# A two-layer graph network on one core: matmul sums parted at other places around transposes, identity products between TensorE's waits, a second copy of layer 1's table, and node rows written later

## The chip, the cores and the metric

The kernel runs on one core of a Trainium2 chip. The metric is the device time of one execution in microseconds (us), as the median of several runs.

## What is computed

A graph of N = 6250 nodes (256 features) and E = 200000 edges, sorted by destination, goes through two graph attention layers (4 heads of 64, then 1 head of 256). Cut to one layer:

```python
te  = relu(edge_attr @ We + be) * exp(x @ Wo + bo)[src][:, None]      # one row per edge
hx  = x @ Wg                                                          # one row per node
al  = leaky_relu((hx·a_s)[src] + (hx·a_d)[dst] + (te @ Wge)·a_e, 0.2)
al  = exp(al - segment_max(al, dst)[dst]); al = al / segment_sum(al, dst)[dst]
out = segment_sum(hx[src] * al, dst) + b                              # also a self loop per node
x   = relu(out + x)            # layer 1: no relu, and the inputs are added once more
```

Layer 1 reads hx of layer 0's result at each edge's source, and a source can be any node: layer 1's first gather needs, in principle, the last node row that layer 0 makes.

## The kernel before

**Steps.** The edges are cut into 66 steps a layer: 64 of 24 chunks of 128 edges, then one of 14 and one of 13. A step covers a window of at most M = 112 consecutive nodes. Its number in the whole run is k (0 to 65 in layer 0, 66 to 131 in layer 1), in its layer s. Within a step:

- `gather` (L941): GpSimd issues one indirect DMA per chunk; it fetches the 128 source rows of the chunk from the layer's table in DRAM, `T[0]` or `T[1]`, into the step's tile G. Three G buffers rotate by k mod 3.
- `rphase1` (L1041, L1042), `rphase2` (L1050), `adst` (L1167), `edge_rows` (L1181): the edges' own term, by TensorE and ScalarE, turned to rows by VectorE.
- `logits` (L1195 to L1212): VectorE adds the terms and scans for maxima; it needs the step's last gather.
- `ends` (L1219), `links` (L1229, L1231, L1236), `maxima` (L1246 to L1272): a small transpose on TensorE, scans across partitions, a transpose back, and the exponentials.
- `scale` (L1303): VectorE multiplies the gathered rows by the weights, in pieces given by `cuts`; `carried` (L1285 to L1293) adds what the step before left over for its last node.
- `onehots` (L1132) and `sums` (L1322): one-hot matrices S, and per chunk one product S x G that accumulates in the PSUM tile u (two matmul instructions a chunk). `evict` (L1327) copies u to U.
- `finish` (L1338 to L1409 in layer 0): merges the self loop, makes the node's new x (tile fb) and, last, in two additions (L1407, L1409), the node row that layer 1 will add to its result.
- `rows1` (two transposes, L1415, and a copy, L1417), `rows2` (the table row's product, L470), `rows3`: VectorE adds the bias (L474), ScalarE takes an exponential (L1427), and SyncE's queue (SP) writes the 112 rows to `T[1]` (L1456), the node rows to `nd` (L1458), and one element to the step before's `nd` (L1461).

**Order.** The schedule is written by hand: instructions run on each engine in the order in which the program lists them, and each waits for its operands and buffers by semaphores. Every step but the last three of a layer goes through the loop in `edges`. The last three (called a, b and c here: 24, 14 and 13 chunks) go through `ending`, in which a's sums stand among b's logits and links, b's sums among c's, and the node rows of a, b and c come last. `after` is the step that follows: the first of layer 1 at the turn, and none at the end of the kernel.

**The turn.** After a's sums, `ending` lets the first step of layer 1 gather already (24 early gathers, L941) from `T[1]`, although the rows of a, b and c are not in it. For the sources that are missing, `lacking` (at k = 4) filled the table's last rows, `sources` loads the list of sources, `select` (L1102, twice) compares it with the numbers of the last 256 nodes, `lack_rows` (L1110) reads these 256 rows of `T[1]` when they are there, and `complete` (L1120, L1121) adds the missing rows to G, 24 pieces of four matmul instructions and one VectorE instruction each. The step after that (k = 67) gathers from the whole `T[1]`; the one after (k = 68) takes a buffer that holds the list and one of the two select matrices until `complete` is done.

**End.** The last two steps of layer 1 write their rows by an indirect DMA of GpSimd (L1469). `flag` sums up the checks of the input (L926 to L930); `general` at the end branches on it.

Of the kernel before, what the change touches and what calls it, by code (L numbers as in the profile page):

```python
# [22 lines left out]
F32 = mybir.dt.float32  # L23
# [8 lines left out]
P = 128  # L32
# [47 lines left out]
class Kernel:  # L80
# [10 lines left out]
    def run(self):  # L91
# [4 lines left out]
        self.T = [self.dp.tile([N + P, L.TW], F32, name=f"T{L.l}") for L in self.L]  # L96
        n, w = (self.NS + 1) // 2, self.L[1].TW + D
# [580 lines left out]
    def edges(self, ctx):  # L678
# [31 lines left out]
        for k, st in enumerate(steps):  # L710
# [63 lines left out]
        self.flag()  # L774
# [8 lines left out]

    def ending(self, a, b, c, pv, late, after):

        nc, k = self.nc, a["k"]
        self.load_lb(k + 3)
# [28 lines left out]
        self.sums(a, (0, n // 3))  # L816
# [7 lines left out]
        self.sums(a, (n // 3, n // 2))  # L824
        self.links(b)
        self.sums(a, (n // 2, n))
        early = after and self.early
# [36 lines left out]
        drain(self.scale(c, cuts=(1, 1 + m // 2, m)))  # L864
# [22 lines left out]
        self.rows2(b)  # L887
        f = self.finish(c)
# [7 lines left out]
        if early:  # L896
            self.select(after, 0)
        self.rows3(c)
        if after:
            fill = iter(())  # L900
            if early:
                self.lack_rows(after)
                self.select(after, 1)
# [5 lines left out]
            for _ in range(C // 3):  # L909
                next(fill, None)  # L910
# [4 lines left out]
            for _ in range(C // 3):  # L915
                next(fill, None)
# [15 lines left out]
    def gather(self, st):  # L932
# [7 lines left out]
        for c in range(0) if st["k"] == 0 and self.CX > last else range(last + 1) if own else (last, *range(last)):  # L940
            nc.gpsimd.indirect_dma_start(  # L941
                out=G[:, c, 0:L.TW], out_offset=None, in_=self.T[L.l][0:self.N, :],
# [130 lines left out]
    def lacking(self):  # L1073
# [4 lines left out]
        for n in (N - 2 * P, N - P):  # L1078
            nc.sync.dma_start(self.T[1][n:n + P, :], none)
# [20 lines left out]
    def select(self, st, j):  # L1100

        self.nc.vector.tensor_tensor(st["sel"][j], st["row"], self.k_lack[:, j:j + 1].to_broadcast([P, C * P]),  # L1102
                                     op=OP.is_equal)
# [210 lines left out]
    def sums(self, st, *parts):  # L1314
        nc, L, c = self.nc, st["L"], st["C"]
        G, S = st["G"], st["S"]
        for a, b in parts or ((0, c),):
            for i in range(a, b):
                j = st["n"] = st.get("n", -1) + 1
                if j == 0:  # L1320
# [54 lines left out]
    def nodes0(self, st, wp, e=None):  # L1375
# [6 lines left out]
        hw = wp.tile([P, D], F32, name="hw", bufs=2)  # L1382
        self.nc.scalar.activation(hw, xw, AF.Relu, bias=tw[:, L.ln + 1:L.ln + 2],
                                  scale=tw[:, L.ln:L.ln + 1])
        st["hw"] = True
# [289 lines left out]
```

## Time and profile before

| | us |
|---|---|
| median of 3 runs | 4016.55 (4015.93 to 4017.98) |
| the profiled execution | 4015.31 |
| its span (first to last instruction) | 4013.5 |
| GpSimd busy in the span | 2998.9 (75%) |
| TensorE matmuls busy | 2655.2 (66%) |
| VectorE busy | 2446.4 (61%) |
| ScalarE busy | 1119.4 (28%) |

PE is TensorE, PEld its weight loads, DVE VectorE, ACT ScalarE, POOL GpSimd, SP SyncE; a "q" behind a name is the engine's queue, which issues DMAs. L941 is line 941 of the kernel. A row of a timeline gives start, duration, engine, line, operation, the tile written and those read, shapes, the number of instructions and, in brackets, the idle time before it with what ended it. A row of waits gives the total, how often, and the longest. In a table by windows, each engine has its busy time and its number of instructions, then come TensorE's granted clock, the DMA engines' share and GB/s. "16 matmuls" below are 16 instructions, 8 chunks.

### The profile page before, as it was taken

To read this page: it belongs to the slowest core of one execution; us is meant where nothing else is said; L and a number is where in the kernel's file an instruction comes from. 1 tells how busy PE (TensorE), PEld (TensorE's weight loads), DVE (VectorE), ACT (ScalarE), POOL (GpSimd) and SP (SyncE) were. 2 spreads that over 40 slices of the span, in tenths; PEclk is the share of its full clock that TensorE was granted. 3 is DMA by queue.
4 is the path that set the end of the run, shared out by engine and by line. 5 is a ranking of instruction groups with operands and counts; after the bars stand their busy time and mean duration, and the time that the engine had idled before them with its cause. 6 is when DMAs were issued, how large, how long until landed. Compare 5 with 4: busy or idle time off the path is not lost.

```text
span 4013.5 us, 37615 instructions
## 1 busy us (share of the span) xinstructions
PE 2655.2 (66%) x9998; PEld 1744.1 (43%) x9998; DVE 2446.4 (61%) x6071; ACT 1119.4 (28%) x2676; POOL 2998.9 (75%) x3264
## 2 busy tenths in 40 slices
PE   8776766766766666666676566566665665665665
PEld 6454444444444444444454343343343343343343
DVE  7898877877877877877874443443443443443445
ACT  6211111111111111111124343343443443443441
POOL 6777777777777777777767777777777777777775
PEclk9888887788888888888888777777777777777777
DMA  7555555555555555555555445445445545545543
GB/s 245 141 160 151 145 154 144 150 154 144 152 154 145 150 154 144 151 155 143 152 155 145 133 138 143 134 137 145 137 134 143 139 132 144 138 132 143 140 131 94
DMA packets 240037, 584.66 MB, mean 146 GB/s; under 512 B 64843, under 2 KB 97265, under 8 KB 239579
## 3 DMA queue, kind: packets, MB, share of 16 engines
q0 software_dynamic: 150144, 422.75, 39.6%
q1 hardware_dynamic: 89133, 159.15, 12.4%
q8 instruction: 86, 1.41, 0.1%
q14 instruction: 130, 1.06, 0.1%
q10 hardware_dynamic: 544, 0.28, 0.0%
HBM read 544.19 MB, written 38.12 MB: 145 GB/s over the span
## 4 chain that ended last, share of the span: by engine, by line
POOL 32%; DVE 28%; issue 14%; PE 11%; ACT 9%; DMA 7%; DVEq 0%; SPq 0%; POOLq 0%; ACTq 0%
POOL G L941 31%; DVE G L1303 8%; ACT G L1312 7%; DMA G<-T,src 7%; PE y L1041 4%; PE u L1322 4%; DVE S L1132 4%; DVE lb L1065 2%; PE ps L470 1%; DVE m L1251 1%; ACT R L1042 1%; DVE rt L1181 1%; DVE al L1199 1%; DVE al L1197 1%; DVE fb L1212 1%
## 5 line engine op out<-in xcount | busy, mean ns | idle before, releaser
L941 POOL DMA_INDIRECT G<-T,src x3102 | 2945.2, 949 | 961.5 <-issue 910.7
L1322 PE MATMUL u<-G,S 128*128 128x270 f32 (+1 forms) x6252 | 1578.4, 415 | 193.3 <-DVE G L1293 190.1
L1322 PEld LDWEIGHTS u<-G,S 128*128 128x128 f32 x6252 | 1284.6, 207 | 487.5 <-DVE G L1293 217.0
L1312 ACT ACTIVATE G<-G,kw 128x256 f32<-128x256 f32 x1512 | 609.0, 497 | 0.0
L1042 ACT ACTIVATE R<-y,webd 128x1024 f32<-128x1024 f32 (+2 forms) x264 | 235.4, 892 | 1275.9 <-PE y L1041 791.4
L1219 PE MATMUL lf<-ident,fb 128*36 128x128 f32 (+1 forms) x132 | 49.6, 376 | 757.5 <-DVE fb L1212 755.6
L1195 DVE TENSOR_TENSOR G<-rt,G 128x96 f32<-128x96 f32 (+1 forms) x132 | 30.4, 230 | 804.7 <-DMA G<-T,src 804.3
L1303 DVE TENSOR_TENSOR G<-G,kps 128x6144 f32<-128x6144 f32 (+3 forms) x77 | 440.9, 5735 | 0.0
L1132 DVE TENSOR_TENSOR S<-kps,loc 128x3072 f32<-128x3072 f32 x132 | 437.7, 3316 | 4.6
L1041 PE MATMUL y<-ea,webd 64*128 64x256 f32 (+1 forms) x1056 | 391.1, 835 | 50.0 <-ACT R L1042 50.0
L1050 PE MATMUL zad<-R,wea 128*64 128x384 f32 (+1 forms) x1056 | 297.6, 704 | 158.6 <-ACT R L1042 158.3
L1219 PEld LDWEIGHTS lf<-ident,fb 128*36 128x36 f32 (+1 forms) x132 | 15.7, 119 | 798.0 <-DVE fb L1212 795.5
L1050 PEld LDWEIGHTS zad<-R,wea 128*64 128x64 f32 x1056 | 85.8, 183 | 420.9 <-ACT R L1042 338.9
L1327 ACT ACTIVATE U<-u 128x270 f32<-128x270 f32 (+1 forms) x132 | 51.8, 393 | 636.8 <-PE u L1322 636.8
L1354 DVE SCALAR_TENSOR_TENSOR mg<-U,mw 128x1 f32<-128x1 f32 x66 | 14.7, 223 | 281.2 <-ACT mw L1352 281.2
L1041 PEld LDWEIGHTS y<-ea,webd 64*128 64x128 f32 x1056 | 123.7, 286 | 122.4 <-ACT R L1042 68.4
L1285 DVE SCALAR_TENSOR_TENSOR G<-U,kw,G 1x257 f32<-1x257 f32 x62 | 29.5, 476 | 183.4 <-ACT G L1312 183.4
L470 PE MATMUL fin<-wg,h1T 128*128 128x260 f32 x264 | 127.6, 634 | 4.3 <-ACT h1T L1417 4.3
L1181 DVE STREAM_TRANSPOSE rt<-zad 128x768 f32<-128x768 f32 (+1 forms) x130 | 126.1, 970 | 4.4 <-PE zad L1167 4.4
L1153 PE MATMUL zad<-a,Q 128*128 128x12 bf16 (+1 forms) x132 | 25.9, 196 | 148.6 <-DVE a L1148 148.2
L1065 DVE TENSOR_TENSOR lb<-lb,kps 128x1536 bf16<-128x1536 bf16 (+1 forms) x68 | 113.0, 1661 | 0.0
L1427 ACT ACTIVATE t1row<-t1row 128x1 f32<-128x1 f32 x66 | 13.4, 203 | 347.1 <-DVE t1row L474 347.1
(225 smaller groups left out, 2303.2 us busy)
## 6 DMA issues: line engine op xcount, KB each, us to landing
G<-T,src POOLq DMA_INDIRECT x3102, 2.8
ea<-in_ea_dram SPq DMA_DIRECT2D x64, 768.0 KB
lb<-locrow SPq DMA_DIRECT2D x64, 384.0 KB
nd<-t1row SPq DMA_DIRECT2D x66, 225.8 KB
tw<-nd SPq DMA_DIRECT2D x66, 225.8 KB
tw<-T SPq DMA_DIRECT2D x66, 117.2 KB
T<-t1row SPq DMA_DIRECT2D x66, 113.8 KB
tw<-in_x_dram SPq DMA_DIRECT2D x66, 112.0 KB
```

The costliest lines, as they stand in the source:

```text
L470: self.nc.tensor.matmul(ps[:, :L.MW], hT[:, k, :], self.wg[L.l][:, k, :], start=(k == 0), stop=(k == 1))
L941: nc.gpsimd.indirect_dma_start(out=G[:, c, 0:L.TW], out_offset=None, in_=self.T[L.l][0:self.N, :], in_offset=bass.IndirectOffsetOnAxis(ap= ...
L1041: nc.tensor.matmul(y[:, i, :n], self.webd[l][r, :], ea[r, w], start=True, stop=True)
L1042: nc.scalar.activation(R[:, :, w], y[:, :, :n], AF.Relu, bias=self.be[l])
L1050: nc.tensor.matmul(st["zad"][i * PH:(i + 1) * PH, o], self.wea[l][0], R[:, i, w], start=True, stop=False)
L1065: V.tensor_tensor(lb[:, :, :n], lb[:, :, :n], self.k_part.unsqueeze(2).to_broadcast([P, i, n]), op=OP.is_equal)
L1132: nc.vector.tensor_tensor(st["S"][:, c0:c1, :], self.k_iota.unsqueeze(1).to_broadcast(w), self.loc[:, o + c0:o + c1].unsqueeze(2).to_broad ...
L1181: V.transpose(rv[:, :32 * c].rearrange("p (b n) -> p b n", b=2), z.rearrange("p (b n) -> p b n", b=2)[:, :, :16 * c])
L1219: self.nc.tensor.transpose(self.lf[0:e.shape[1], 1:P + 1], e, self.ident)
L1303: nc.vector.tensor_tensor(v, v, pw[:, c0:c1, :].unsqueeze(3) .to_broadcast([P, c1 - c0, H, L.F]), op=OP.mult)
L1312: self.nc.scalar.activation(v, v, AF.Copy, scale=st["w"][:, c:c + 1])
L1322: nc.tensor.matmul(st["u"][:, :L.W], S[:, i, :], G[:, i, 0:L.W], start=(j == 0), stop=(j == c - 1))
```

## The change

1. A second table `T1` in DRAM gets the same rows as `T[1]` from every step of layer 0 but the last three, by one more DMA a step. The early gathers read `T1`; the filling of its last rows moves to it too.
2. In the turn's `ending`, the two additions that make a node row (`node_x`) and the two writes to `nd` (`rows4`) of a, b and c move behind the table rows, in among the pieces of `complete`.
3. `sums` of a are parted at 10 chunks (before: 8) around b's `ends`, those of b at 8 and 10 (before: 11) around c's `ends` and `links`; `scale` of c is cut at 1, 3 and 8 (before: 1 and 7). At the kernel's end, c's sums get a PSUM tile of their own.
4. In the turn, 10 products of the identity with itself (128 x 512, into a u tile that nobody reads) are put at five places of TensorE's order: 1, 1, 2, 2 and 4.
5. The first `select` before c's table row covers 16 of 24 chunks; the rest comes behind it. `complete`'s pieces are spread 2, 2, 2, 6 and 12 (before: 8, 8 and 8).
6. `flag` runs in step 2 of layer 1 (before: last).
7. The buffers of three small tiles: hw 3 (2), fa 1 (2), fb 3 (2).

```diff
+        self.T1 = self.dp.tile([N + P, self.L[1].TW], F32, name="T1e")
...
+            if st["L"].l and (st["s"] == 2 or st["s"] + 3 == self.NS) and not hasattr(self, "flag_i"):
+                self.flag()
...
-        self.flag()
...
+    def warm(self, n, pool, name, shape):
+
+        t = pool.tile(shape, F32, name=name)
+        t = (t[:, 0, :] if len(shape) > 2 else t).rearrange("p (k n) -> p k n", k=4)
+        for _ in range(n):
+            self.nc.tensor.matmul(t, self.ident, self.ident.unsqueeze(1).to_broadcast([P, 4, P]), start=True, stop=True)
...
     def ending(self, a, b, c, pv, late, after):
...
+        early = after and self.early
+        for q in (a, b, c) if after else ():
+            q["lag"] = True
...
         self.load_ea(k + 2)
+        if after:
+            self.warm(1, self.ps_1, "u", [P, 512])
         self.rphase2(b)
         self.adst(b)
         self.rows1(pv)
+        if after:
+            self.warm(1, self.ps_1, "u", [P, 512])
         drain(self.scale(a))
         self.carried(a)
         n = a["C"]
         self.rows2(pv)
-        self.sums(a, (0, n // 3))
+        if after:
+            self.warm(2, self.ps_1, "u", [P, 512])
+        p = 5 * n // 12
+        self.sums(a, (0, p))
         self.rows3(pv)
...
-        self.sums(a, (n // 3, n // 2))
+        self.sums(a, (p, n // 2))
         self.links(b)
         self.sums(a, (n // 2, n))
...
+            after["from"] = self.T1
             self.gather(after)
...
         m = c["C"]
-        self.sums(b, (1, n - 3))
+        p, q = min(n, n // 2 + 1), min(n, n // 2 + 3)
+        self.sums(b, (1, p))
         self.edge_rows(c)
         drain(self.logits(c))
         self.ends(c)
+        self.sums(b, (p, q))
         for _ in range(3):
             next(f)
         self.links(c)
-        self.sums(b, (n - 3, n), (0, 1))
+        self.sums(b, (q, n), (0, 1))
...
-        drain(self.scale(c, cuts=(1, 1 + m // 2, m)))
+        if not after:
+            c["u"] = self.ps_f.tile([P, 512], F32, name="fin")
+        drain(self.scale(c, cuts=(1, min(3, m), 2 + m // 2, m)))
         drain(self.scale(c, cuts=(0, 1)))
...
         self.rows1(b)
         self.rows2(b)
+        if after:
+            self.warm(2, self.ps_1, "u", [P, 512])
         f = self.finish(c)
...
         if early:
-            self.select(after, 0)
+            self.select(after, 0, 0, 16)
         self.rows3(c)
         if after:
             fill = iter(())
             if early:
                 self.lack_rows(after)
+                self.warm(4, self.ps_1, "u", [P, 512])
+                self.select(after, 0, 16)
                 self.select(after, 1)
                 fill = self.complete(after)
             else:
                 self.gather(after)
             self.nodes(after)
             self.spread(after)
-            for _ in range(C // 3):
-                next(fill, None)
+            for q in (a, b, c):
+                for _ in range(C // 12):
+                    next(fill, None)
+                drain(self.node_x(q))
+                self.rows4(q)
             self.parts(after)
             self.blocks(after)
             self.rphase2(after)
             self.adst(after)
-            for _ in range(C // 3):
+            for _ in range(C // 4):
                 next(fill, None)
             self.edge_rows(after)
             drain(fill)
...
-                out=G[:, c, 0:L.TW], out_offset=None, in_=self.T[L.l][0:self.N, :],
+                out=G[:, c, 0:L.TW], out_offset=None, in_=st.get("from", self.T[L.l])[0:self.N, :],
...
-            nc.sync.dma_start(self.T[1][n:n + P, :], none)
+            nc.sync.dma_start(self.T1[n:n + P, :], none)
...
             nc.sync.dma_start(self.T[1][ds(r, M), :], t[1:M + 1, :L1.TW])
-            n = s // 2 * (M + 1)
-            nc.sync.dma_start(self.nd[s % 2][n:n + M, :], t[1:M + 1, :])
-            if s:
-                n = self.row(2, s - 1)
-                nc.sync.dma_start(self.nd[(s - 1) % 2][ds(n, 1), L1.ad:L1.ad + 1], t[1:2, L1.ad:L1.ad + 1])
+            if self.early and s + 3 < self.NS:
+                nc.sync.dma_start(self.T1[ds(r, M), :], t[1:M + 1, :L1.TW])
+            if "lag" not in st:
+                self.rows4(st)
             return
```

`rows4` holds the lines that left `rows3`; `node_x` holds the two additions that left `nodes0`, which still makes them at once for steps without the mark `lag`.

More of the change, by code (lines that the diff above doesn't have):

```diff
@@ L1098, in sources, with select @@
         st["sel"] = [self.sp.tile([P, C, P], F32, name="S").rearrange("p c e -> p (c e)"), X[:, n:2 * n]]
[L1100 to L1103 removed]
+    def select(self, st, j, c0=0, c1=C):
+        w = slice(P * c0, P * c1)
+        self.nc.vector.tensor_tensor(st["sel"][j][:, w], st["row"][:, w],
+                                     self.k_lack[:, j:j + 1].to_broadcast([P, P * (c1 - c0)]), op=OP.is_equal)
     def lack_rows(self, st):
@@ L1319, in sums @@
                 j = st["n"] = st.get("n", -1) + 1
-                if j == 0:
+                if j == 0 and "u" not in st:
                     st["u"] = self.ps_1.tile([P, 512], F32, name="u")
@@ L1433, in nodes1 @@
         yield from self.merge(st, wp, w)
-        st["o"] = o = wp.tile([P, D], F32, name="fb")
+        st["o"] = o = wp.tile([P, D], F32, name="fb", bufs=3)
         V.scalar_tensor_tensor(o, U[:, 0:D], w[:, 0, 0:1], xw, op0=OP.mult, op1=OP.add)
@@ L1471, in rows3, with rows4, node_x @@
                 in_offset=None, bounds_check=self.N - 1, oob_is_err=False)
+    def rows4(self, st):
+        nc, s, t, L1 = self.nc, st["s"], st["trow"], self.L[1]
+        n = s // 2 * (M + 1)
+        nc.sync.dma_start(self.nd[s % 2][n:n + M, :], t[1:M + 1, :])
+        if s:
+            n = self.row(2, s - 1)
+            nc.sync.dma_start(self.nd[(s - 1) % 2][ds(n, 1), L1.ad:L1.ad + 1], t[1:2, L1.ad:L1.ad + 1])
+    def node_x(self, st, e=None):
+        e = e or self.nc.vector
+        nrow = st["trow"][:, self.L[1].TW:self.L[1].TW + D]
+        e.tensor_add(nrow, st["xw"], st["hw"])
+        yield
+        e.tensor_add(nrow, nrow, st["x1"])
+        yield
     def general(self):
```

18 lines of the change are left out of this document (7 added, 11 removed).

## The prediction

> **What bounds the kernel now.** I read the page's groups first, then the windows of line L941, and only then the timelines of the turn and of the end.
>
> ```profile
> L941 POOL DMA_INDIRECT G<-T,src x3102 | 2945.2, 949 | 961.5 <-issue 910.7
> ```
>
> 3102 gathers of 0.949 us, with 0.3 us of issue before nearly every one. The windows, of these instructions alone, cut the span where they pause:
>
> ```profile
> 82.70:2047.75 1965.05, 1487.96 (x1563) 0.83 0.55 151
> 2047.75:2056.82 9.07, 0.01 (x2) 0.50 0.42 129
> 2056.82:3982.49 1925.67, 1457.19 (x1539) 0.73 0.50 138
> 3982.49:4013.50 31.01, 0.00 (x0) 0.78 0.07 16
> ```
>
> 1965.05 / 1563 = 1.257 us a gather, 1925.67 / 1539 = 1.251: GpSimd issues without a pause in both layers. So the time is a start of 82.7 us, two streams of gathers, a hole of 9.07 us at the turn and a tail of 31.0 us. What the change does elsewhere counts only if it shortens the hole or the tail, or makes the stream wait.
>
> The hole, in GpSimd's timeline, SP's waits between 2035 and 2065 us and SP's timeline:
>
> ```profile
> 2046.59 1.16 POOL L941 DMA_INDIRECT G<-T,src  x1 [0.30 <-issue]
> 2056.82 0.94 POOL L941 DMA_INDIRECT G<-T,src  x1 [9.06 <-DVE Q L1066]
> ```
>
> ```profile
> SPq L1456 <- DMA G<-T,src: 12.1, 3, 7.2
> ```
>
> ```profile
> 2049.83 0.33 SPq L1456 DMA_DIRECT2D T<-t1row  x1
> ...
> 2054.14 0.32 SPq L1456 DMA_DIRECT2D T<-t1row  x1
> ```
>
> The first names VectorE's Q, but no gather reads Q. The second tells what happened: a's table row waits until the early gathers, which read the same table, have landed; it goes out at 2049.83, and c's, behind b's and the node rows, at 2054.14. The gather that reads the whole table starts 2.68 us behind that. Unhindered it would start 0.30 after 2047.75, at 2048.05.
>
> **The change, part by part.**
>
> *The second table* takes that wait away: nothing reads T[1] before the whole-table gather. What is then late is c's row itself, in VectorE's and TensorE's timelines:
>
> ```profile
> 2046.51 0.42 DVE L1407 TENSOR_TENSOR t1row<-tw,hw 128x256 f32<-128x256 f32 x1
> 2047.08 0.43 DVE L1409 TENSOR_TENSOR t1row<-t1row,fb 128x256 f32<-128x256 f32 x1
> 2047.42 3.35 DVE L1102 TENSOR_TENSOR S<-G,kps 128x3072 f32<-128x3072 int32 x1
> 2050.68 0.42 DVE L474 TENSOR_TENSOR t1row<-fin,bias 128x260 f32<-128x260 f32 x1
> ```
>
> ```profile
> 2040.47 1.13 PE L1041 MATMUL y<-ea,webd 64*128 64x512 f32 x4
> 2042.10 0.41 PE L1415 MATMUL fin<-ident,fb 128*128 128x128 f32 x2 [0.50 <-DVE cnt L1338]
> 2043.52 1.14 PE L470 MATMUL fin<-wg,h1T 128*128 128x260 f32 x4 [1.01 <-ACT h1T L1417]
> 2047.10 0.69 PE L1415 MATMUL fin<-ident,fb 128*128 128x128 f32 x2 [2.43 <-ACT fb L1401]
> 2048.32 2.10 PE L470 MATMUL fin<-wg,h1T 128*128 128x260 f32 x4 [0.53 <-ACT h1T L1417]
> ```
>
> c's addition (L474) starts at 2050.68; with an estimated 0.8 for itself, the exponential and SP, its row could go out at 2051.5, had nothing else changed. The copy's price: 63 more writes on SP, each with an issue of 0.33 us like the row above, ahead of nd and of later loads; SP waits for other engines most of each step, which hides them (uncovered, 0.33 a step). On the DMA engines I bound it by the two streams: 1487.96 / 1563 = 0.952 us a gather in layer 0, which has four transfers a step that layer 1 lacks (both tw loads, T, nd), 0.947 in layer 1. 24 x 0.005 = 0.12 us a step, so 0.03 for one more, or 1.9 us in all; a gain has no reason. I take 0: the DMA share of 0.55 leaves room.
>
> *Sums parted, with identity products.* The chain of work, then VectorE and TensorE around b's transpose, then the windows with the granted clock:
>
> ```profile
> 2003.01 6.42 PE u L1322 x16
> 2009.55 1.93 PE u L1322 x8
> 2011.66 5.68 PE u L1322 x24
> ```
>
> ```profile
> 2007.59 0.24 DVE L1212 TENSOR_TENSOR_SCAN fb<-pen,al 128x56 f32<-128x56 bf16 x1
> ...
> 2009.27 0.27 PE L1219 MATMUL lf<-ident,fb 128*36 128x128 f32 x1
> ```
>
> ```profile
> 1996.00:2003.00 7.00, 4.78 (x16) 2.49 (x16) 6.97 (x6) 1.08 (x2) 5.36 (x6) 0.50 0.59 158
> 2003.00:2008.00 5.00, 4.99 (x11) 3.84 (x12) 4.79 (x12) 0.20 (x1) 3.78 (x5) 0.50 0.61 175
> 2008.00:2017.00 9.00, 9.00 (x41) 7.03 (x40) 6.25 (x13) 0.22 (x1) 6.87 (x8) 0.99 0.42 113
> ```
>
> A sums instruction takes 6.42 / 16 = 0.40 us at first and 5.68 / 24 = 0.24 later; the clock stays at half through 5 us of full work. b's scans end at 2007.83, its transpose waits for the sums until 2009.27. The turn has no identity product; by the sums' rates it takes 2 x 0.24 x 512 / 270 = 0.9 us at full clock and twice that, 1.8, at half: an estimate, with these as its ends, and I take 1.8 for the first. Counted from 1996: 1.8, then 2.7 (4.78 without the table row's 2.10): the clock comes up at about 2000.5. A product at 0.9, the table row at 1.14, two products at 1.8: sums start at 2004.4 instead of 2003.01, and their 20 instructions end at 2009.2. So b's transpose gains nothing; behind it 4 instructions stand instead of 8, and about 0.6 us comes out. At c:
>
> ```profile
> 2023.98 0.24 DVE L1212 TENSOR_TENSOR_SCAN fb<-pen,al 128x52 f32<-128x52 bf16 x1
> ```
>
> ```profile
> 2021.02 4.75 PE L1322 MATMUL u<-G,S 128*128 128x270 f32 x20
> 2025.61 0.27 PE L1219 MATMUL lf<-ident,fb 128*36 128x128 f32 x1
> ```
>
> With 14 instructions instead of 20, c's transpose comes 1.4 us sooner, at its scans' end (2024.22); three small operations of VectorE's keep 0.3 of that, so the links and all behind them gain 0.6 + 1.1 = 1.7. The finer cuts of scale cost one instruction more, 0.1.
>
> *Node rows late* take two additions of 0.4, 0.8 together, from behind each finish. a's and b's come out ahead of a's L474, which gains 1.6 + 0.8 + 0.8 = 3.2 us. Behind it comes layer 1's edge term (the L1041 row: 1.13, and as much on ScalarE), which follows TensorE and holds 0.4 back: b's L474 gains 2.8. The two products behind b's L470 (1.8) end before c's transposes and keep the clock up, so these take 0.41 instead of 0.69 and c's L470 1.14 instead of 2.10. It now ends at 2048.32 + 2.10 = 2050.42; then at 2050.42 - 2.8 - 0.28 - 0.96 = 2046.4. The select's 16 of 24 chunks (2.23 us) follow c's finish, without its additions at 2046.6 - 2.8 = 2043.8, and end by 2046.1, in time. c's L474 starts at 2046.45, its row goes out at 2047.25, the gather 2.68 later, at 2049.9: **the hole falls from 9.07 to 2.15 us, a gain of 6.9**. Bounds: 8.77 (a hole of 0.30), and 5.2, if parting and products bring nothing (c's L474 at 2050.68 - 1.6 - 1.2 = 2047.9, the gather at 2051.4).
>
> *What is late next*: the buffer of k = 68. The gathers of k = 67 last 24 x 1.25 = 30 us, then to 2080; complete must be done by then. Its first and last products now, in TensorE's timeline and in the chain:
>
> ```profile
> 2058.31 1.21 PE L1120 MATMUL y<-U,S 128*128 128x260 f32 x2 [7.89 <-DMA U<-T]
> ```
>
> ```profile
> 2084.79 0.89 PE u L1120 x4
> ```
>
> It ends at 2085.7, 1.1 us before 2056.82 + 30. In the new order the last rows are read 6.9 us earlier; until about 2061 the first six pieces share VectorE with the rest of the select, the spread and six additions, then 18 pieces of 0.88 on TensorE end at 2077: 3 us of cover. The four products behind c's row lie in a wait for that read. nd's writes, behind that read on SP, make the node loads of k = 67 and 68 wait until about 2061; these are needed after complete: nothing.
>
> *The end*, VectorE and TensorE:
>
> ```profile
> 3985.58 0.17 DVE L1212 TENSOR_TENSOR_SCAN fb<-pen,al 128x13 f32<-128x13 bf16 x1
> ```
>
> ```profile
> 3981.63 5.98 PE L1322 MATMUL u<-G,S 128*128 128x261 f32 x20
> 3987.45 0.27 PE L1219 MATMUL lf<-ident,fb 128*33 128x128 f32 x1
> ...
> 3992.24 5.96 PE L1322 MATMUL u<-G,S 128*128 128x261 f32 x26 [1.32 <-ACT U L1327]
> ```
>
> 14 instructions end at 3985.8, with the scans: links and scale gain 1.4. c's sums, in a tile of their own and with two chunks scaled first, start when b's end (3990.05) and end at 3996.0 instead of 3998.2. VectorE, with b's merge, then sets the end, 1.85 us earlier. **The tail gains 1.85** (bounds 0.5, if c's sums are held up by their scale, and 2.2). a's parting at 10 holds b's transpose by 0.6 and gives it back behind. flag's operations stood beside the last write: nothing. fa's one buffer has only VectorE for reader and writer: no wait.
>
> **Sum**: 6.9 + 1.85 = 8.75 us off 4015.31 gives 4006.6 for a profiled execution; the median of the runs stands 1.24 above it, so 4007.8.
>
> **The rivals.**
>
> *A, products in the way.* If the clock comes up 2 us later than I put it, one more product and the table row run at half: sums start 1 to 2 us later still, b's transpose comes over 1 us later than now, and the hole's gain falls to some 5.7: 4009.0. For it speaks that 4.78 us of work in 7 lifted nothing; against it, that the new order leaves no holes. [...]
>
> *B, complete bounds.* If complete runs beyond 2080 (VectorE's additions between its pieces), GpSimd waits at k = 68, one for one. The cover is 1.1 us now, 3 by my sum; 2 us too late gives 4009.8.
>
> *C, the hole closes wholly*: c's row out 1.85 us earlier than I have it, as when the products let the sums start at 2003.0: 4016.55 - 8.77 - 1.85 = 4005.9.
>
> *D, slower: the copy stretches the stream.* Place: layer 0's 63 steps. The gains are used up at 8.75 / 63 = 0.14 us a step, slower by 0.2% needs (8.75 + 8.0) / 63 = 0.27; with 0.3, a quarter of a gather, 4016.55 - 8.75 + 18.9 = 4026.7. Against it stand the 0.12 us that four such transfers cost.
>
> That the change doesn't do what it says would show as SP's L1456 waiting for gathers still: the tail alone, 4014.7; the early gathers name another table, so I give it 0.01.
>
> **How the numbers follow.** Forecast (4006.3 to 4009.3) 0.54; C 0.16; A 0.15; B 0.10; D 0.04; nothing done 0.01. A measurement of this kernel can tell about 0.2%, 8.0 us, from no change: below 4008.5 is faster. The forecast lies there three times in four (0.40), C always (0.16), A now and then (0.02): faster 0.58, same 0.38, slower 0.04. The range reaches from C with a tail of 2.2 and 0.7 for runs that differ to A and B with as much of the copy's 1.9: 4004.8 to 4012.0.
>
> **What would show it.** Right: one GpSimd wait of 1 to 3 us in the turn, SP's L1456 waiting for ScalarE alone, c's L470 at 1.14 us, the granted clock near 1 from 2004 on, c's last copy 2 us nearer the last gather. Wrong: a second long wait at k = 68 (B), b's transpose later than now (A), layer 0's gathers over 0.96 us in the mean (D).

## The result, and the profile after

| us | before | changed |
|---|---|---|
| median of 20 runs | 4017.36 (4013.26 to 4019.48) | 4009.32 (4003.33 to 4012.03) |
| profiled execution, and its span | 4015.31, 4013.5 | 4009.49, 4007.7 |
| hole of the gather stream at the turn | 9.07 | 2.54 |
| from the last gather to the end | 31.0 | 27.6 |

The ratio of the times is 0.998, 95% interval 0.9974 to 0.9986: 8.0 us, 0.2%. The forecast was 4007.8, its range 4004.8 to 4012.0.

Line numbers have moved: gathers L971, sums L1353, table product L471, its addition L475, row write L1484, read of the last rows L1141, identity products L791 (in the kernels of the experiments they differ by a few lines more). The windows of the gathers alone, cut as for the kernel before:

```profile
82.63:2050.66 1968.03, 1488.51 (x1563) 0.83 0.57 154
2050.66:2053.20 2.54, 0.00 (x1) 1.00 0.50 126
2053.20:3980.06 1926.86, 1458.36 (x1539) 0.74 0.51 139
3980.06:4007.70 27.64, 0.00 (x0) 0.81 0.06 19
```

The reader is to see four things. The hole lost 6.5 us. The tail lost 3.4. The gathers' own time is as it was (1488.5 against 1488.0 us in layer 0). And layer 0's stretch is 3.0 us longer for the same 1563 gathers. In both kernels GpSimd waited twice in it for more than the 0.3 us of issue: at 113 us for 0.85 (before: 0.95), and again for the buffer that the second step's sums read, where the wait grew. That second row, and the sums of the first step behind it, in this kernel and then in the kernel before:

```profile
176.92 0.94 POOL L971 DMA_INDIRECT G<-T,src  x1 [3.40 <-PE fin L1443]
...
139.07 13.48 PE L1353 MATMUL u<-G,S 128*128 128x270 f32 x48 [0.95 <-DVE G L1334]
```

```profile
174.39 0.94 POOL L941 DMA_INDIRECT G<-T,src  x1 [0.87 <-PE fin L1415]
...
138.72 11.21 PE L1322 MATMUL u<-G,S 128*128 128x270 f32 x48 [0.96 <-DVE G L1303]
```

The same 48 instructions took 13.48 us instead of 11.21, part of them at half clock: the granted clock was 0.50 until 143.7 us here and until 137.6 in the kernel before. This lies far ahead of the turn. Hole (-6.5), tail (-3.4), this wait (+2.5) and 1.6 us more of stream elsewhere make -5.8, the difference of the two spans. The medians differ by 8.0 because the profiled execution of the kernel before lies 2.05 us under its median, and that of the changed kernel 0.17 above its own.

At the turn, VectorE's addition of c's table row, SP's last row write and the read that waits for it, and the gathers around the hole:

```profile
2048.62 0.43 DVE L475 TENSOR_TENSOR t1row<-fin,bias 128x260 f32<-128x260 f32 x1 [0.46 <-PE fin L471]
```

```profile
2049.31 0.32 SPq L1484 DMA_DIRECT2D T<-t1row  x1
2052.42 0.84 SPq L1141 DMA_DIRECT2D U<-T  x2
```

```profile
2049.71 0.95 POOL L971 DMA_INDIRECT G<-T1e,src  x1 [0.30 <-issue]
2053.20 0.94 POOL L971 DMA_INDIRECT G<-T,src  x1 [2.54 <-DMA T<-t1row]
```

SP's waits in the turn:

```profile
SPq L1484 <- ACT t1row L1455: 5.5, 2, 3.6
SPq L1484 <- DMA T<-t1row: 5.3, 2, 3.5
```

The early gathers read T1e, and no row write waits for them any more, only for ScalarE and for the landing of the write before. c's addition starts 2.04 us ahead of their end at 2050.66; before, it stood 2.93 behind it (2050.68 against 2047.75). The row goes out at 2049.31. What ends the hole is its landing: 3.11 us from issue to the read that waits for it, where the forecast had 1.9 and 0.8 behind that.

TensorE around a's sums, with the two windows of the granted clock:

```profile
2003.90 1.88 PE L791 MATMUL u<-ident 128*128 128x512 f32 x4
2006.21 4.80 PE L1353 MATMUL u<-G,S 128*128 128x270 f32 x20 [0.43 <-PE u L791]
2011.05 0.30 PE L1250 MATMUL lf<-ident,fb 128*36 128x128 f32 x1
```

```profile
1996.00:2003.00 7.00, 7.00 (x24) 3.15 (x25) 6.66 (x9) 1.92 (x5) 5.19 (x6) 0.67 0.60 160
2003.00:2008.00 5.00, 4.57 (x17) 2.90 (x17) 4.90 (x10) 0.20 (x1) 3.78 (x4) 1.00 0.60 154
```

The clock is full from 2003 on, where it was 0.50 until 2008; the sums take 0.24 us each from the first, and b's transpose no longer waits for them.

At the end, VectorE's scan, TensorE's transpose behind it, c's last sums in their own tile, and the last write:

```profile
3983.20 0.17 DVE L1243 TENSOR_TENSOR_SCAN fb<-pen,al 128x13 f32<-128x13 bf16 x1
```

```profile
3983.42 0.30 PE L1250 MATMUL lf<-ident,fb 128*33 128x128 f32 x1 [1.32 <-DVE fb L1243]
...
3988.61 5.11 PE L1353 MATMUL fin<-G,S 128*128 128x261 f32 x22 [0.25 <-DVE G L1334]
```

```profile
3997.69 1.00 POOL L1496 DMA_INDIRECT out_dram<-fb,oidx  x1 [2.15 <-DVE fb L1465]
```

The transpose now follows the scans at once (before: 1.7 us behind them). From the last write to the end of the span it is 10.0 us instead of 11.6 (4013.50 - 4001.88), and the forecast has no term for that.

### The profile page after: what moved, and what is told of

Same layout as the page of the kernel before. It is cut to its first block, busy times and chain, and to the rows that moved or that the text cites. A ratio compares the mean times of both kernels' runs of the same rounds, so it can differ in the third digit from the quotient of the medians.

```text
span 4007.7 us, 37932 instructions
## 1 busy us (share of the span) xinstructions
PE 2654.4 (66%) x10018; PEld 1741.3 (43%) x10018; DVE 2446.4 (61%) x6074; ACT 1120.2 (28%) x2676; POOL 3000.5 (75%) x3264
## 5 line engine op out<-in xcount | busy, mean ns | idle before, releaser
L971 POOL DMA_INDIRECT G<-T,src x3078 | 2923.8, 950 | 949.6 <-issue 898.1
L1353 PE MATMUL u<-G,S 128*128 128x270 f32 (+1 forms) x6226 | 1567.4, 415 | 192.1 <-DVE G L1324 190.7
L1353 PEld LDWEIGHTS u<-G,S 128*128 128x128 f32 x6226 | 1275.5, 206 | 483.3 <-DVE G L1324 217.4
L1080 PE MATMUL zad<-R,wea 128*64 128x384 f32 (+1 forms) x1056 | 301.7, 712 | 157.8 <-ACT R L1072 157.6
L1080 PEld LDWEIGHTS zad<-R,wea 128*64 128x64 f32 x1056 | 86.5, 185 | 418.0 <-ACT R L1072 333.7
L1316 DVE SCALAR_TENSOR_TENSOR G<-U,kw,G 1x257 f32<-1x257 f32 x62 | 29.6, 477 | 184.3 <-ACT G L1343 184.3
L471 PE MATMUL fin<-wg,h1T 128*128 128x260 f32 x264 | 122.6, 611 | 3.6 <-ACT h1T L1445 3.6
```

The source lines that it names most:

```text
L471: self.nc.tensor.matmul(ps[:, :L.MW], hT[:, k, :], self.wg[L.l][:, k, :], start=(k == 0), stop=(k == 1))
L971: nc.gpsimd.indirect_dma_start(out=G[:, c, 0:L.TW], out_offset=None, in_=st.get("from", self.T[L.l])[0:self.N, :], in_offset=bass.Indirect ...
L1080: nc.tensor.matmul(st["zad"][i * PH:(i + 1) * PH, o], self.wea[l][0], R[:, i, w], start=True, stop=False)
L1353: nc.tensor.matmul(st["u"][:, :L.W], S[:, i, :], G[:, i, 0:L.W], start=(j == 0), stop=(j == c - 1))
```

## The experiments

My theory, from the traces: at the turn, two chains run side by side, the early gathers' landing with the row writes behind it, and c's row, and the later of them ends the hole; the second is set by TensorE's clock. The rivals were that one part of the change does all, and that the products hold the sums up. A hole is the bracket of GpSimd's row at the turn, a tail the time behind the last gather, both from one profile of each kernel. Times are compared with the kernel before in runs on the same chip; the changed kernel stands at 0.9982 (0.9973 to 0.9991) in the last set. One execution of each was profiled, and it need not be a typical one: with the table alone and without the products it was the shortest of 11, 7.0 and 8.3 us under the median.

**The table alone** (kernel before, plus):

```diff
+        self.T1 = self.dp.tile([N + P, self.L[1].TW], F32, name="T1e")
+            if self.early and s + 3 < self.NS:
+                nc.sync.dma_start(self.T1[ds(r, M), :], t[1:M + 1, :L1.TW])
+            after["from"] = self.T1
```

> The kernel before with the second table alone (copy of every row but the last three steps', early gathers read it); sums, products, node rows, flag and end as before. If SP's wait for the early gathers held the first 2 to 3 us of the hole and c's own row the rest (the prediction's account): the three rows go out unhindered, c's addition stays 2.9 us behind the end of the early gathers, its row goes out 0.8 later and the gather 2.68 behind that: hole 6.4 instead of 9.07, tail 31.0, 2.7 us off the time. Rival: the table removes the whole hole by itself (0.3). Rival: it removes nothing (9.07), since the rows are late anyway.

```profile
2055.11 0.95 POOL L943 DMA_INDIRECT G<-T,src  x1 [5.07 <-DMA T<-t1row]
```

Hole 5.07, tail 29.9. The timed runs tell nothing of it: ratio 0.9998, 0.9989 to 1.0007, an interval that reaches down to 4.4 us, where the profile's hole is 4.0 shorter. In the profiled execution the clock had come up early (the table product ahead of a's sums took 1.14 us instead of 2.10), so that c's addition stood 1.68 us behind the early gathers instead of 2.93. So the table was tried once more, with the early flag:

```diff
+            if st["L"].l and (st["s"] == 2 or st["s"] + 3 == self.NS) and not hasattr(self, "flag_i"):
+                self.flag()
...
-        self.flag()
```

> The kernel before with the second table and the flag's early place; sums, products and node rows as before. By the profiles of the two parts: hole 5.1 instead of 9.07, tail 1.2 less: 5.2 us less than the kernel before. Rival, by the timed runs of the table alone (0.5 us above the kernel before, interval -4.4 to 2.8): the shorter hole is given back elsewhere: 1.2 us less or nothing, and a stall stands later in its trace.

```profile
2055.76 0.94 POOL L944 DMA_INDIRECT G<-T,src  x1 [6.52 <-DMA T<-t1row]
```

Hole 6.52, against the 6.4 worked out for it; in this run c's addition again starts 2.93 us behind the early gathers. Ratio 0.9993 (0.9984 to 1.0002), 2.8 us: no stall stands later in the trace, so nothing is given back, but the time alone would not tell it from nothing. Of the two profiles this one is nearer to its kernel's median (0.6 us under it), so 2.5 us is the better figure for the table alone.

**All but the table** (changed kernel, the same lines taken out, `lacking` filling T[1] again):

> The changed kernel with the second table taken out: early gathers read layer 1's own table, no copies; all else as changed. Theory: SP's row write waits again until the early gathers have landed (2.1 us behind the last of them in the kernel before), the three rows follow at 0.5 us each without node rows between, gather 2.68 behind the third: hole 5.8 instead of 2.54, tail 27.65, time 3.3 us above the changed kernel. Rival, the table is all of the gain at the turn: hole 9.07 again, time 6.5 above. Rival, the table is worth nothing once the rows are early: 2.5.

```profile
2054.79 0.33 SPq L1482 DMA_DIRECT2D T<-t1row  x1
2056.87 0.33 SPq L1482 DMA_DIRECT2D T<-t1row  x1
2058.86 0.32 SPq L1482 DMA_DIRECT2D T<-t1row  x1
2060.83 0.84 SPq L1139 DMA_DIRECT2D U<-T  x2
```

```profile
2061.60 0.95 POOL L969 DMA_INDIRECT G<-T,src  x1 [8.92 <-DMA T<-t1row]
```

Hole 8.92; I expected 5.8. The three row writes stand 2.0 to 2.1 us apart, although all three rows were ready and nothing lay between them on SP. SP's waits name the reason, the landing of the write before:

```profile
SPq L1482 <- DMA T<-t1row: 3.0, 2, 1.5
```

So without the table the chain is 2.1 us of landing, three writes of 2.0 and 0.8 to the gather, whatever VectorE and TensorE do: the rest of the change is worth nothing at the turn (8.92 against 9.07), although c's addition came 4.7 us sooner behind a's scale (50.6 us instead of 55.3). With the table, the rest is worth 6.5 - 2.5 = 4.0 (2.5 by the lower of the two holes with the table alone). The time does not speak against it: 0.9994 (0.9985 to 1.0003), where the shorter tail alone would give 0.9992.

**No identity products** (changed kernel; `for _ in range(n)` in `warm` becomes `range(0)`):

> The changed kernel without its identity products; all else as changed. Theory (products lift the clock at no cost to the sums): a's first 20 sums run at half clock again, 8.0 us instead of 4.8, b's transpose and all behind it comes 1.5 to 3 us later, c's transposes and table product take 0.69 and 2.10 instead of 0.44 and 1.15: hole 5 to 7 us instead of 2.54. Rival A of the prediction (products in the way): hole 2.5 or shorter, a's sums start earlier. The tail stays at 27.65 either way.

```profile
2005.58 7.30 PE L1353 MATMUL u<-G,S 128*128 128x270 f32 x20 [0.85 <-DVE G L1324]
...
2045.08 2.10 PE L471 MATMUL fin<-wg,h1T 128*128 128x260 f32 x4 [0.87 <-ACT h1T L1445]
...
2050.84 2.10 PE L471 MATMUL fin<-wg,h1T 128*128 128x260 f32 x4 [0.53 <-ACT h1T L1445]
```

```profile
2056.32 0.94 POOL L971 DMA_INDIRECT G<-T,src  x1 [5.94 <-DMA T<-t1row]
```

Hole 5.94, within 5 to 7. a's sums take 7.30 instead of 4.80 and b's and c's table products 2.10 instead of 1.15. Rival A falls: with and without products, a's sums start 7.6 us behind the start of a's scale, so that the products cost them nothing. The ratio is 0.9991 (0.9982 to 1.0).

**The old parting at the turn:**

```diff
-        p = 5 * n // 12
+        p = n // 3 if after else 5 * n // 12
-        p, q = min(n, n // 2 + 1), min(n, n // 2 + 3)
+        p = q = n - 3          # at the end as changed
```

> The changed kernel with the turn's sums parted where they were (a's behind a third, b's three from the end); the end and all else as changed. The prediction's step: b's transpose 0.6 later, c's 1.1 more, together 1.7: hole 4.2 instead of 2.54. By the trace of the changed kernel, where b's transpose stands 1.7 us better against VectorE's scale than before, up to 2.8: hole 5.3. Rival: c's row is set by VectorE's other work: hole 2.5. Tail 27.65.

```profile
2042.44 2.10 PE L471 MATMUL fin<-wg,h1T 128*128 128x260 f32 x4 [0.86 <-ACT h1T L1447]
```

```profile
2052.58 0.95 POOL L973 DMA_INDIRECT G<-T,src  x1 [6.09 <-PE u L791]
```

**The old node rows** (the lines that set `lag`, and `node_x` and `rows4` among the pieces of `complete`, taken out):

> The changed kernel with the last three steps' node rows where they were (two additions in each finish, two writes behind each table row); all else as changed. The prediction's step: 0.8 us each for a's and b's, hole 4.1; with SP's node writes ahead of c's row as much as 5. Rival: they lie in VectorE's waits for ScalarE and TensorE: hole 2.5. Tail 27.65.

```profile
2042.93 2.10 PE L471 MATMUL fin<-wg,h1T 128*128 128x260 f32 x4 [0.87 <-ACT h1T L1441]
```

```profile
2053.36 0.95 POOL L967 DMA_INDIRECT G<-T,src  x1 [5.13 <-PE u L791]
```

Holes 6.09 and 5.13, ratios 0.9987 (0.9978 to 0.9996) and 0.9988 (0.9979 to 0.9997). Both are more than the prediction's 4.2 and 4.1, and the undone parts together (3.4 for the products, 3.6 for the parting, 2.6 for the rows) make more than the 4.0 that they are worth. The table products show a reason: in both kernels the clock was down at b's product (2.10 us instead of 1.15), with the identity products in place. By the time, neither can be told from the changed kernel.

**The changed kernel again:**

> The changed kernel once more, beside the three others on one chip, as their measure. One gather hole of 2.54 us in its first profile; the kernels with the same turn gave 1.1 to 3.7. Expected 1 to 4 us, tail 27.7, 8 us less than the kernel before.

```profile
2042.83 2.10 PE L471 MATMUL fin<-wg,h1T 128*128 128x260 f32 x4 [0.86 <-ACT h1T L1445]
```

```profile
2053.05 0.94 POOL L971 DMA_INDIRECT G<-T,src  x1 [4.00 <-DMA T<-t1row]
```

Without any edit the clock falls here too, and the hole is 4.00. Over the six profiles with this same turn, the holes are 2.54, 2.27, 1.16 and 1.13 where the clock stayed up, 4.00 where b's product took 2.10, and 3.70 in the one of the old end (below), where the clock was down from a's product to b's transposes and c's last gathers landed 1.8 us late: mean 2.5.

A difference of two holes is still no price of a part, since a hole also holds where the early gathers happen to end. Counted from the start of a's scale, which lies ahead of all that the parting and the late rows change:

| us behind the start of a's scale | a's row addition | c's row addition | end of the early gathers | hole |
|---|---|---|---|---|
| kernel before | 46.15 | 55.30 | 52.37 | 9.07 |
| changed | 41.83 | 50.07 | 52.11 | 2.54 |
| changed, again | 43.08 | 52.95 | 52.32 | 4.00 |
| no products | 43.67 | 55.02 | 52.43 | 5.94 |
| old parting | 43.56 | 53.43 | 50.77 | 6.09 |
| old node rows | 43.43 | 53.23 | 51.49 | 5.13 |

Up to a's addition the clock was the same in the changed kernel, with the old parting and with the old rows: there the parting is worth 1.7 us and the late rows 1.6, as predicted (1.7 and 1.6). From there to c's addition it is 8.2 us with the clock up and 9.8 to 9.9 in the three profiles in which it fell. What else lengthens the two holes is early gathers that ended 1.3 and 0.6 us sooner, which neither edit can have caused, since GpSimd waits for nothing there; a landing of c's row that was 1.2 us shorter takes some of it off. The products are worth 1.8 at a's addition and 4.9 at c's: without them, in a profile with the clock down at b's product too, parting and late rows together bring c's addition forward by only 0.3.

**The flag last, and the old parting at the end:**

```diff
-            if st["L"].l and (...) and not hasattr(self, "flag_i"):
-                self.flag()
+        self.flag()            # behind the loop
```

> The changed kernel with the flag's product, sum and test back behind the last step; all else as changed. The prediction's step: nothing, tail 27.65. Theory now: in the kernel before 4.5 us lie between the last write of the output and its landing, in the changed one 2.6, and it is the flag that is read beside it: tail 29.0 to 29.6. Rival: the difference is the last write's own and comes with the sums' own PSUM tile: tail 27.65.

```profile
3981.70:4010.50 28.80, 0.01 (x1) 0.80 0.07 17
```

```profile
3999.30 1.00 POOL L1495 DMA_INDIRECT out_dram<-fb,oidx  x1 [2.15 <-DVE flag_i L959]
```

```diff
-        p = 5 * n // 12
+        p = 5 * n // 12 if after else n // 3
+        # and b's sums parted at n - 3 where there is no step after
```

> The changed kernel with layer 1's sums parted where they were; flag, own tile and cuts and the turn as changed. The prediction's step: links and scale 1.4 us later: tail 29.05. By the trace of the changed kernel, c's copy of the p column stands 1.5 us nearer the last gather: 29.15. Rival: the end is set by VectorE's merges alone: 27.65. Hole 2.54.

```profile
3982.74:4010.50 27.76, 0.00 (x1) 0.83 0.06 18
```

```profile
3981.65 4.59 PE L1355 MATMUL u<-G,S 128*128 128x261 f32 x20
3986.08 0.28 PE L1252 MATMUL lf<-ident,fb 128*33 128x128 f32 x1
```

The flag is worth 1.2 us in the changed kernel (tail 28.80, a little under the 29.0 to 29.6 expected): the last write starts at the same distance from the last gather (17.6 us) in both, and the end comes 1.2 later. The parting at the end, from which I expected 1.4, is worth 0.1. With the old parting the 20 sums took 4.59 us here, at full clock, and were done when the scans were; in the profile of the kernel before they took 5.98. Both tails with the old parting and full clock, 29.9 with the table alone and 27.76 here, differ by 2.1: 1.2 is the flag by the price above, and 0.9 is left. The last write starts 17.91 us behind the last gather with the table alone and 17.59 here, so c's own PSUM tile and the finer cuts, which I did not take apart, show 0.3 of it; the rest lies behind that write, and the table with the early flag, tail 28.52, makes the flag worth 1.4. A tail moves by as much with the clock alone: with the old node rows, an edit at the turn, it was 28.57 for an expected 27.65, ten of b's last sums taking 4.15 us instead of 2.47. The ratios, 0.9984 (0.9975 to 0.9993) and 0.9981 (0.9972 to 0.999), can't tell either from the changed kernel.

**Three copies instead of one:**

```diff
-                nc.sync.dma_start(self.T1[ds(r, M), :], t[1:M + 1, :L1.TW])
+                for x in (self.T1, *self.T2):
+                    nc.sync.dma_start(x[ds(r, M), :], t[1:M + 1, :L1.TW])
```

> The changed kernel with three copies of every table row instead of one (two more tables that nothing reads). The prediction's step: 0.03 us for a transfer and step at most, so 0 to 3.8 us for the 126 more, all of it in longer gathers of layer 0; layer 0's sum of gather times stays within 4 us of the changed kernel's. Rival D: 0.3 us a copy and step, 38 us more. Rival: the writes wait for one another on SP and push loads back: a stall of the gathers in every step of layer 0.

```profile
84.02:2051.12 1967.10, 1488.19 (x1563) 0.84 0.60 162
2052.28:3978.00 1925.72, 1457.31 (x1539) 0.74 0.51 139
```

1488.19 us for layer 0's gathers with 189 copies, 1488.51 with 63, 1487.96 in the kernel before, with none: a copy costs nothing that can be seen. Rival D falls. The ratio is 0.9979 (0.997 to 0.9988).

**Products ahead of the first steps' sums:**

```diff
         self.adst(steps[0])
+        self.warm(2, self.ps_1, "u", [P, 512])
...
+            if k == 1:
+                self.warm(2, self.ps_1, "u", [P, 512])
             if st["rows"]:
```

> The changed kernel with two identity products more behind the first step's last small product, and two ahead of the second step's sums, both in waits of TensorE of 3.2 to 3.5 us. Theory (the gather stream's wait of 3.40 us at 176.9 is the sums of the first two steps at half clock): both steps' 48 sums take 11.2 us, the wait falls to under 0.9 or goes, the time falls by 2.5 to 3 us against the changed kernel's profile, and the runs, which spread over 8.7 us, come closer together. Rival (that wait is a matter of transfers): wait and spread as they are.

```profile
138.21 11.21 PE L1356 MATMUL u<-G,S 128*128 128x270 f32 x48 [1.35 <-DVE G L1337]
160.67 11.18 PE L1356 MATMUL u<-G,S 128*128 128x270 f32 x48 [1.44 <-issue]
```

The wait of the gathers is gone (0.30 before each of them there), ratio 0.9974 (0.9964 to 0.9985), 10.5 us below the kernel before. So the wait was the clock's: it is 0.87 us in the kernel before, 3.40 and 1.94 in the two profiles of the changed one and 3.41 with the old end, all without these products, and 0.30 in both kernels with them. The eight runs spread over 5.1 us where the changed kernel's 20 spread over 8.7; fewer runs spread less, so that is a hint at most. The last kernel adds two edits at the turn to this:

```diff
         self.rows1(a)
+        if after:
+            self.warm(2, self.ps_y, "y", [P, 2, 512])
         self.rows2(a)
...
-        drain(y)
...
         self.rows3(c)
+        drain(y)
```

> The changed kernel with identity products ahead of the first two steps' sums, two more between a's transposes and its table product, and layer 1's second edge term moved behind c's row. Theory (at the turn the clock falls in TensorE's 2 us wait for a's copy, in some runs, and ScalarE's edge term holds c's merge back by up to 0.85 us): c's table product always 1.15 us, c's addition 2.4 to 3.2 us ahead of the end of the early gathers instead of 2.0 or less, hole under 1.5, no wait at 176.9; 3 to 5 us less than the changed kernel on this chip. Rival: the products hold c's chain up as much as the clock gives: hole 2 to 3.5, 2.5 us less in all.

```profile
2036.80 1.88 PE L794 MATMUL y<-ident 128*128 128x512 f32 x4
2038.93 1.14 PE L471 MATMUL fin<-wg,h1T 128*128 128x260 f32 x4 [0.25 <-ACT h1T L1450]
...
2041.63 1.15 PE L471 MATMUL fin<-wg,h1T 128*128 128x260 f32 x4 [0.53 <-ACT h1T L1450]
```

```profile
2051.45 0.94 POOL L976 DMA_INDIRECT G<-T,src  x1 [2.49 <-DMA T<-t1row]
```

Median 4007.43 (4004.36 to 4008.50) against 4009.42 (4003.72 to 4012.94) of the changed kernel on the same chip; ratio to before 0.9978 (0.9968 to 0.9987). That gain is not shown: the kernel with three copies, which has nothing to make it faster, has 4007.45 on that chip. What is left is the spread, 4.1 us against 9.2 and 7.0. The clock stayed up through the turn, as meant, though it did so in four of the six profiles without the edits at the turn. The hole, 2.49, isn't under 1.5: c's addition came 1.46 us ahead of the early gathers' end, not 2.4 or more, since in this run the gathers stood 1.5 us earlier against a's scale than in the changed kernel's (1998.55 to 2050.66); c's addition itself came 0.9 us sooner behind it (49.1 instead of 50.1). Why that distance differs from run to run, by up to 2.8 us, stays open.

## Why the prediction was right, point by point

The median, 4009.32, lies in the range and 1.5 us above the forecast; sign and places were right. Part of that is luck. By the two profiles the gain was 5.8 us for a forecast of 8.75: the tail gave 1.5 more than forecast, by terms that were put at nothing, and 4.1 us of wait and stream in layers 0 and 1 were not in the forecast. A hole of one profile is no close test either, with 1.1 to 4.0 us in six of the same turn. And the median stands nearer to the numbers of rivals A (4009.0) and B (4009.8) than to the forecast's 4007.8; what rules these two out is not the time but the traces, as said below. Point by point:

- *The second table takes SP's wait away, and c's row is late next*: right, and shown by both kernels with the table (6.52 in the one with the old clock, for 6.4). But the sign that SP's row writes would wait for ScalarE alone did not come: they waited 5.5 us for it and 5.3 for the landing of the write before. And the reason given for the 9.07 us was too short. I put the distance between a's and c's writes down to the node rows on SP's queue; the kernel without the table has none between them, and they stand as far apart (4.1 us, before 4.3), since each write waits for the landing of the one before (SP waited 3.0 us for it there). Hence table and rest are not two gains to be added: each shows only with the other.
- *Sums start at 2004.4 instead of 2003.01, nothing gained at b*: the clock came up at 2000.6, near the 2000.5 that I had estimated from 4.5 us of work ahead of it (L1080, behind the first identity product, took 0.98 us at 2000.83), but the start was not delayed: 7.66 us behind the start of a's scale, before 7.63. That is also why rival A falls; no run shows the 2 us by which A has the clock come up later. So b's transpose came 1.4 us sooner against that scale, where the forecast had no gain. The clock alone did that: with the old parting the transpose stands as early (12.38 us behind the scale, 12.50 with the new one). At c the parting is worth 1.8 us (29.30 and 27.50).
- *c's addition ahead of the early gathers' end by 2047.75 - 2046.45 = 1.3*: it was 2.0, and 0.3 to 2.4 in the other profiles with this turn, except 0.6 behind it in the one with the fallen clock at b.
- *The gather 2.68 us behind the row's write*: the step that failed. It was read from a write with no gathers in flight. In the kernel before that write took 1.90 from issue to the read that waits for it (2054.14 to 2056.04); with the early gathers still landing it took 3.11. Why so much stays open: in the two kernels whose rows went out 0.3 us sooner still, ahead of the same gathers, it was 2.05. With 1.90 the hole would have been 1.3; c's row, 0.7 us earlier than forecast, made good some of the 1.2 us lost.
- *The tail gains 1.85 by parting, own tile and cuts; the flag nothing*: failed in size and cause. 3.4 was measured. The flag is 1.2 to 1.4 of it, the parting 0.1 where the clock is full (where it isn't was not measured), and about 1.1 of the 31.0 us was a clock that fell just then in the profile of the kernel before.
- *GpSimd issues without a pause in both layers*: there were two short pauses in layer 0, 0.95 and 0.87 us, and the second grew to 3.40 with the clock. The forecast has no term for it.
- *The copy costs nothing*: right, with three copies too.
- *Rival B, complete bounds*: GpSimd waited no more than 0.30 us at k = 68 in the profiles of the changed kernel and of the one without products. But `complete` did not end at 2077: it ended at 2084.8, 1.3 us after the gathers of k = 68 had begun (2083.48), and 1.7 after without the products. By the forecast's own rule that is a wait. It was none because, by `sources`, the list fills about the first 11 chunks of that buffer and the select matrix the next 11: the gathers overwrite them chunk by chunk, and reach the matrix 14 us (11 gathers of 1.25) behind their first.
- *Rival C*, the hole closed wholly: not so in any run, but 1.13 and 1.16 are near to it.

So the 8.0 us between the medians come from the hole (6.6, with 2.5 as the mean of six profiles, but 9.07 from one), the flag (1.2) and what else the end gained beside the clock (0.9). That makes 8.7; the 0.7 over is less than single profiles differ by, and the sum is an estimate for that reason.

## What to carry to other kernels

Where an engine that sets the time waits for the later of two chains, take the parts of a change out one by one, and never add their worths: here the table without the rest gave 2.5 to 4 us of the hole, the rest without the table 0.15, both 6.5. Price a part by one chain, from an instruction ahead of the edit to one behind it, and not by a wait, which also holds where the other chain happens to stand. In this kernel the writes to one table, at rows known only at run time, waited for each other's landing (2.0 to 2.1 us apart without the second table), and a's row for that of the early gathers until they had a table of their own (hole 6.52 instead of 9.07 by the table and the early flag): chains that no engine's busy time shows. And a price for TensorE read from one profile may hold half a clock that the next run doesn't have (b's table product took 1.14 us in one profile of the changed kernel and 2.10 in the other): read the same instructions in several profiles before a term rests on them.

## What the runs showed of the hardware

**The clock fell in one profile and stayed up in another behind the same work.** The same stretch of work ahead of the end, in the profile of the kernel before and of the changed one (columns as in the prediction's windows; PE's busy time comes first, the granted clock third from the end):

```profile
3977.60:3981.20 3.60, 2.12 (x17) 1.09 (x16) 2.91 (x9) 1.60 (x3) 2.80 (x3) 0.98 0.39 106
3981.20:3985.20 4.00, 4.00 (x14) 3.16 (x13) 1.75 (x8) 0.30 (x1) 0.98 (x2) 0.59 0.28 75
```

```profile
3975.00:3978.60 3.60, 2.12 (x17) 1.09 (x16) 2.89 (x7) 1.61 (x3) 2.69 (x4) 1.00 0.41 106
3978.60:3982.10 3.50, 3.50 (x18) 2.68 (x16) 1.25 (x5) 0.30 (x1) 1.15 (x2) 1.00 0.35 95
```

TensorE was busy for 2.12 of 3.60 us in both, with no wait over 0.8, and then for all of the next stretch; in one the clock fell to 0.59, in the other it stayed at 1. Cut where the clock changes, the windows give it more sharply: in the kernel before, TensorE was busy for 1.93 us, 57%, from 3977.62 to 3981.03 at a clock of 1.00, which was 0.50 from there to 3984.45 and 1.00 again from 3984.45 to 3987.86; in the changed kernel it was busy for 80, 77 and 61% of the three stretches of that length from 3973.48 on, and the clock was 1.00 from 3966.65 to 3997.37. At the turn it is alike: in the changed kernel TensorE was busy for 2.54 of the 4.50 us from 2036.80 and for 2.48 of the 3.60 behind them, both at 1.00; in its second profile for 2.57 of the 4.50 us from 2036.70, with a clock of 0.89 in them and of 0.50 in the 3.60 from 2041.20. So nearly the same busy time went with either clock. That it depends on where a wait lies against the clock's changes is my estimate from these numbers, and was not shown. In the last kernel, with identity products in a wait of 2 us, TensorE was busy for 3.54 of the 4.40 us from 2036.50 and the clock was 1.00; one profile does not show that they did it.

**A row's landing while the early gathers land.** From the issue of c's row to the read that waits for it: 1.89 to 1.97 us in the seven profiles in which the row went out 1.3 us or more behind the end of the last early gather (the kernel before, the changed one again, and those with the table alone, without the table, without products, with the old parting and with the old rows); 2.05, 2.05, 2.39, 2.55, 2.83 and 3.11 in the six in which it went out up to 1.7 ahead of that end or 0.4 behind it (three copies, products ahead of the first steps, the last kernel, the old end, the flag last, the changed kernel). The two rows that went out earliest, 1.7 us ahead of the end, are those that took 2.05, so the order of the two is not all of it; what sets the time was not shown.

**Executions differ by as much as the change, and not by the chip alone.** The kernel before has a median of 4024.45 us on one chip and 4015.77 on another. On the first, the gathers alone took longer in the profile without the table (1491.80 and 1462.38 us in the two streams, against 1488.19 and 1457.31 in the kernel with three copies on a third chip). But on that first chip one execution of the kernel without products, at 4012.91 us, was 5.0 us shorter than any other of its 11. Comparisons across chips would have hidden all of the 8 us; what sets the gathers' time stays open.
